# A two-layer gated MLP on one core: new order of first loads, filler transposes, a joint last block, and the last 96 features as one product

## The chip, the core and the metric

The kernel runs on one core of a Trainium2 chip. The core has five engines with instruction streams of their own: TensorE (PE, matrix products and transposes, with its weight loads shown apart as PEld), VectorE (DVE), ScalarE (ACT), GpSimd (POOL) and SyncE (SP). In this kernel SP issues every load and store, one after the other. Sums of products grow in PSUM banks, all other tiles lie in SBUF, and inputs, outputs and some intermediate arrays lie in DRAM.

The metric is the device time of one execution in microseconds (us), as a median over several runs. Besides these runs one execution is recorded by the profiler, and its rows are what "the profile" and "the trace" mean below.

## The reference, cut to what matters

The input x is 2048 tokens by 512 features (4 x 512 tokens). Two layers follow one another, and each adds to x the layer norm of what it computes from the layer norm of x.

```
def _L0_attn_ref(x, w_gate, w_up, w_down):
    s = silu(x @ w_gate.T)                       # 1376 features
    k = int(0.5 * I)
    _, idx = top_k(-abs(s), k)                   # the 688 smallest in magnitude of each row
    s[rows, idx] = 0
    s = s * (x @ w_up.T)
    return s @ w_down.T                          # back to 512

def _L0_ffn_ref(x, W_gate, W_up, W_down):
    return (silu(x @ W_gate.T) * (x @ W_up.T)) @ W_down.T

x = x + layernorm(_L0_attn_ref(layernorm(x), ...))
x = x + layernorm(_L0_ffn_ref(layernorm(x), ...))
```

All is in f32. The first layer thus needs, for each token, the median of 1376 magnitudes, and sets to zero what lies below it; the second layer has no such step.

## The kernel before, in words

Tokens are in 16 tiles of 128. The 1376 features are 10 groups of 128 and a last group of 96; the name `I` is 1376, `HF` is 640, so `2 * HF` is where the last 96 begin.

**Products with seven multiplications.** Most products are not made plainly. A product of matrices cut into 2 x 2 parts can be made with seven part products, where eight would be plain, if certain sums of parts are made first. `Seven` (L132) does that for products whose sums over the features are in PSUM: `first` makes products p1, p6, p5 in the banks pa, px, py; pa is copied out and px is added to the copy; `second` adds p7 to px and p2 to pa; `third` adds p4 to px and p3 to py. Because the banks go on being summed up, the copies and additions between these steps have to come in order. `stationary_sums` (L116) and `moving_sums` (L124) make the sums of parts for the side that TensorE holds and for the side that streams through it. `downs` (L233) does the same for the products with the down weights, with ten groups of 128 as two halves of five: its steps are p1, p5, p6 for each pair of tiles, then p7, p2, p4, p3, where each of the seven needs its own right side of 640 KB, loaded by `down_right` into a ring of three buffers. The last 96 features are added in `rest` (L263) by a plain matmul, for p7 in a bank of its own. Sums of weights that the second layer and the down products need are made once, early, by `presum` (L179), and lie in DRAM.

**Layer 1** (`Unit`, L348) goes by eight units of two tiles. For a unit, x is loaded and normalized, transposed on TensorE and copied out of PSUM by ScalarE (`normed_T`, L339); the gate product is made plainly in three column pieces of 464, 456 and 456 (L404), each followed on ScalarE by Silu (L408) and the magnitude (L409); the up product is a `Seven`. Then the threshold is searched: six passes of ScalarE over a tile with Sign and a sum (L456), each followed by small steps on VectorE, and an exact end (to L516). The masked product p is transposed on TensorE (`turns`, L578) and copied out by ScalarE (L582, L584), and then `downs` runs. These stages are offset: while unit j makes its gate and up products, unit j-1 is searched, unit j-2 is transposed and unit j-3 does its down products. `out_norm` (L321) takes statistics of the finished rows (`moments`, L98, ending with a power of -0.5 on POOL, L109), subtracts and scales on VectorE, adds x on POOL (L331) and stores.

**Layer 2** (`Block`, L624) goes by four blocks of four tiles. A block has five calls of `pair` (gate and up of 256 features, both as `Seven`), then `rest` (L674): gate and up of the last 96 features, 4 matmuls of 512 columns each into one bank for gate and one for up, Silu on ScalarE and a product on VectorE (L686). POOL makes the sums for the down products (`down_sums`). Then `finish` runs `downs` for the block's two pairs of tiles. In blocks 0 to 2 both pairs share a call, so that each right side is loaded once; in block 3 the first pair is finished, and then the second, each with its own seven loads. In the last call `final=True` lets `out_norm` take its statistics in two halves and do the last scaling and the addition of x in one instruction of VectorE (L328).

**The layer change** is where the two last units of layer 1 are searched, transposed and finished while the first block of layer 2 starts: the norms of block 0's first tiles and the loads of layer 2's weights are placed between the steps of unit 6 and unit 7. At its end a count of rows for which the search was not exact (`badi`) is made; after all work, every engine reads this count (L875) and jumps over a second, slower version of the whole computation (L876).

**What sets the order.** The code above is emitted in the order in which it is written, in `layers` (L721). Inside the block that L873 opens, a scheduler then orders each engine's instructions by its own estimate of times and dependences, so an edit at one place can reorder instructions at another. Buffers come from pools with a fixed number each: two PSUM banks for each of the tags pa, px, py and pt, three for the ring of down weights. At the start, 18 transposes of a constant (`warm`) run on TensorE before the first data is there.

## Time and profile before

| | us |
|---|---|
| three runs | 886.12, 888.31, 889.33 |
| median | 888.31 |
| the profiled execution | 887.46 |
| its span, first to last record | 885.5 |
| TensorE busy in it | 862.3 |
| VectorE, ScalarE, POOL busy | 511.8, 300.9, 180.3 |
| mean granted clock of TensorE | 0.993 |
| data moved | 117.54 MB |

The span is the time between the first and the last record of the profile; the device time of the same execution is 1.96 longer. An f32 matmul shows as two records, one after the other, because TensorE goes over f32 data in two passes; where a "pass" is spoken of, one record is meant. The granted clock is the share of full speed that TensorE was allowed in a stretch of time. "Waits" are idle times of an engine, put down to the instruction or transfer that released it. In a row such as `PE pg L404 <- ACT p L408: 2.5, 1, 2.5` TensorE waited at line 404 (output tile pg) for ScalarE's line 408 (output tile p), 2.5 us in sum, once, at most 2.5.

### The profile page before, as it was taken

To read this page: it belongs to the slowest core of one execution; us is meant where nothing else is said; L and a number is where in the kernel's file an instruction comes from. 1 tells how busy PE (TensorE), PEld (TensorE's weight loads), DVE (VectorE), ACT (ScalarE), POOL (GpSimd) and SP (SyncE) were. 2 spreads that over 40 slices of the span, in tenths; PEclk is the share of its full clock that TensorE was granted. 3 is DMA by queue.
4 is the path that set the end of the run, shared out by engine and by line. 5 is a ranking of instruction groups with operands and counts; after the bars stand their busy time and mean duration, and the time that the engine had idled before them with its cause. 6 is when DMAs were issued, how large, how long until landed. Compare 5 with 4: busy or idle time off the path is not lost. (4 is left out here: it accounts for less than half of the span.)

```text
span 885.5 us, 10211 instructions
## 1 busy us (share of the span) xinstructions
PE 862.3 (97%) x3588; PEld 652.4 (74%) x3588; DVE 511.8 (58%) x1328; ACT 300.9 (34%) x598; POOL 180.3 (20%) x249
## 2 busy tenths in 40 slices
PE   8999999999999899999999999999999999999995
PEld 5656566757667576677788888888788888888784
DVE  4887776775939578766955434554236443444322
ACT  2465575748463757466011111011101112011100
POOL 2120111212212112110433211321203221122221
PEclk9999999999999999999999999999999999999998
DMA  9999413334232343377374003610045002420064
GB/s 317 360 335 345 165 54 119 120 101 143 78 119 98 103 138 102 119 293 262 132 254 150 0 1 113 195 44 0 30 143 167 1 0 65 143 97 1 30 217 156
DMA packets 62924, 117.54 MB, mean 133 GB/s; under 512 B 4816, under 2 KB 36560, under 8 KB 62864
## 3 DMA queue, kind: packets, MB, share of 16 engines
q1 hardware_dynamic: 62864, 116.80, 39.4%
q8 instruction: 30, 0.49, 0.2%
q14 instruction: 30, 0.25, 0.1%
HBM read 97.91 MB, written 18.87 MB: 132 GB/s over the span
## 5 line engine op out<-in xcount | busy, mean ns | idle before, releaser
L456 ACT ACTIVATE ja<-v,cur 128x1376 bf16<-128x1376 f32 x96 | 138.3, 1441 | 76.9 <-DVE cur L481 54.4
L404 PE MATMUL pg<-wg,xT 128*128 128x456 f32 (+1 forms) x384 | 158.0, 559 | 3.4 <-ACT p L408 2.5
L404 PEld LDWEIGHTS pg<-wg,xT 128*128 128x128 f32 x384 | 73.2, 193 | 68.6 <-issue 59.9
L118 POOL TENSOR_TENSOR D<-hTb 128x256 f32<-128x256 f32 x20 | 14.6, 730 | 180.5 <-DVE hTb L672 180.5
L461 DVE TENSOR_SCALAR low<-cur 128x2 int32<-128x2 f32 x48 | 8.7, 181 | 72.0 <-ACT ja L456 72.0
L143 PE MATMUL pau<-wu,xT 128*128 128x344 f32 x128 | 43.6, 452 | 0.0
L143 PE MATMUL pagb<-xTb,wg 128*128 128x256 f32 x160 | 41.4, 379 | 0.0
L143 PE MATMUL paub<-xTb,wu 128*128 128x256 f32 x160 | 41.3, 380 | 0.0
L143 PE MATMUL pxub<-T,wu 128*128 128x256 f32 x160 | 41.2, 380 | 0.0
L143 PE MATMUL pxgb<-T,wg 128*128 128x256 f32 x160 | 41.1, 379 | 0.0
L258 PE MATMUL pad<-wd_p,hT 128*128 128x256 f32 x160 | 39.4, 380 | 1.3 <-DMA wd_p<-in_L_attn_w_down_dram 1.3
L408 ACT ACTIVATE p<-pg 128x456 f32<-128x456 f32 (+1 forms) x48 | 26.0, 544 | 43.1 <-PE pg L404 39.5
L258 PE MATMUL pxdb<-wdb_p,hTb 128*128 128x256 f32 x160 | 36.7, 379 | 2.1 <-DMA wdb_p<-sum_f 2.1
L258 PE MATMUL pxd<-wd_p,hT 128*128 128x256 f32 x160 | 37.2, 380 | 1.5 <-DVE y L293 1.5
L258 PE MATMUL padb<-wdb_p,hTb 128*128 128x256 f32 x160 | 37.1, 379 | 0.9 <-DMA wdb_p<-in_L_ffn_W_down_dram 0.9
L258 PE MATMUL pydb<-wdb_p,D 128*128 128x256 f32 x160 | 37.9, 379 | 0.1
L258 PEld LDWEIGHTS pxd<-wd_p,hT 128*128 128x128 f32 x160 | 30.3, 190 | 7.4 <-DVE y L293 1.7
L258 PEld LDWEIGHTS padb<-wdb_p,hTb 128*128 128x128 f32 x160 | 30.3, 190 | 7.2 <-issue 3.3
L258 PEld LDWEIGHTS pxdb<-wdb_p,hTb 128*128 128x128 f32 x160 | 30.3, 190 | 6.7 <-issue 2.5
L258 PEld LDWEIGHTS pad<-wd_p,hT 128*128 128x128 f32 x160 | 29.6, 190 | 7.4 <-DMA wd_p<-in_L_attn_w_down_dram 1.7
L258 PEld LDWEIGHTS pydb<-wdb_p,D 128*128 128x128 f32 x160 | 30.1, 190 | 6.2 <-issue 2.5
L670 ACT ACTIVATE sg<-sg 128x768 f32<-128x768 f32 x20 | 16.9, 843 | 50.9 <-DVE sg L167 50.9
(221 smaller groups left out, 1721.9 us busy)
## 6 DMA issues: line engine op xcount, KB each, us to landing
wd_p<-sum_a SPq DMA_DIRECT2D x28, 640.0 KB, 4.0
wd_p<-in_L_attn_w_down_dram SPq DMA_DIRECT2D x21, 640.0 KB, 4.2
wdb_p<-sum_f SPq DMA_DIRECT2D x20, 640.0 KB, 4.1
wdb_p<-in_L_ffn_W_down_dram SPq DMA_DIRECT2D x15, 640.0 KB, 4.2
xn<-in_x_dram SPq DMA_DIRECT2D x16, 256.0 KB, 3.1
xr<-in_x_dram SPq DMA_DIRECT2D x16, 256.0 KB, 2.8
x<-y SPq DMA_DIRECT2D x16, 256.0 KB, 2.0
xnb<-x SPq DMA_DIRECT2D x16, 256.0 KB, 3.1
```

The lines of the kernel that those rows point to most:

```text
L118: eng.tensor_add(s1, a21, a22)
L143: nc.tensor.matmul(ps, self.left[k][:, c, :], self.right[k][:, c, :], start=first and c == 0, stop=c == 1, skip_group_check=not first,)
L258: nc.tensor.matmul(p[which], p[1](k, c), ws[k][:, c, :], start=first and c == 0, stop=c == HC - 1, skip_group_check=not first,)
L404: nc.tensor.matmul(pg, self.xT[:, i, c, :], wg[:, c, c0:c1], start=(c == 0), stop=(c == NH - 1),)
L408: nc.scalar.activation(p[:, c0:c1], pg, AF.Silu)
L456: nc.scalar.activation(junk, v, AF.Sign, bias=cur[:, 0, i : i + 1], accum_out=cur[:, 1, i : i + 1],)
L461: nc.vector.tensor_scalar(low, cur[:, 1, :], 0.0, None, ALU.is_gt)
L670: nc.scalar.activation(sg[:, 1:, :], sg[:, 1:, :], AF.Silu)
```

## The change

There are six parts.

1. *First loads.* SP's order was x of tile 0, x of tile 1, and three column pieces of the gate weights. It becomes tile 0, the first piece, tile 1, and the two other pieces. Six filler transposes of tile 0's data, whose results nobody reads, are emitted after tile 0's norm.
2. *Order of sums in `downs`.* The addition of px (product p7) to yb's upper half is emitted right after p7, where it was emitted after p2; the rest of that sum becomes a step of its own, `c22`.
3. *Last block.* Its two pairs are made in one call of `downs`. The order of its end is p7, c22, p3, and then p4 and p2 of the first pair, p4 and p2 of the second. The last tile's `out_norm` takes its statistics for the first half straight from the PSUM bank of the p2 product and subtracts the mean by halves.
4. *The last 96 features.* Gate and up become one `Seven`: its 2 x 2 parts are gate and up on one side, two halves of the 512 input features, and two halves of the block's 512 tokens on the other. Its 14 matmuls have 256 columns. Three sums of the 96-column weights, made once on VectorE at the layer change (four instructions), go with it.
5. *Copies of transposed tiles.* For the unit before the last (`other`), the copies out of PSUM for its second tile go to VectorE in place of ScalarE.
6. *The count.* The read of `badi` and the jump are written inside the scheduled block. The read on SP thereby comes to stand in the layer change, after the load of x for tile 14's `out_norm` and before the load of tile 7 for layer 2; the other engines read it at their ends, as before.

With other edits the scheduler's estimate changes too, and the order in the middle of layer 1 is not the same as before, though none of its lines was edited.

```diff
-    def moments(src, nm, kind, n=1):
+    def moments(parts, nm, kind):
+        n = len(parts)
...
-        for i in range(n):
-            nc.vector.bn_stats(st[:, i, :], src[:, ts(i, H // n)])
+        for i in reversed(range(n)):
+            nc.vector.bn_stats(st[:, i, :], parts[i])
...
-        def product(k, which, i=None):
+        def product(k, which, i=None, part=slice(None)):
...
-            for p in [st[i]] if first else st:
+            for p in [st[i]] if first else st[part]:
...
         def p7():
             product("p7", PX)
             for p in st:
+                tiles, left, last, pa, px, py, ya, yb = p
+                nc.vector.tensor_add(yb[:, hi], yb[:, lo], px)
                 pz.append(bank("pt", f"pz{nm}_{p[0][0]}")[:, :H2])
                 rest(pz[-1], p, 1, hi, True)
 
-        def p2():
-            product("p2", PA)
+        def c22():
             for p, z in zip(st, pz):
                 tiles, left, last, pa, px, py, ya, yb = p
-                rest(pa, p, 0, lo)
-                nc.vector.tensor_add(yb[:, hi], yb[:, lo], px)
                 nc.vector.tensor_add(yb[:, hi], yb[:, hi], py)
                 nc.vector.tensor_add(yb[:, hi], yb[:, hi], z)
-                nc.scalar.copy(ya[:, lo], pa)
...
+        def p2(part=slice(None)):
+            product("p2", PA, None, part)
+            for p in st[part]:
+                tiles, left, last, pa, px, py, ya, yb = p
+                rest(pa, p, 0, lo)
+                if not final:
+                    nc.scalar.copy(ya[:, lo], pa)
+            if not final:
+                c22()
+            else:
+                for p in st[part]:
+                    tiles, left, last, pa, px, py, ya, yb = p
+                    if p is st[-1]:
+                        out_norm(work, tiles[0], ya, res, dst, nm, pa)
+                    else:
+                        nc.scalar.copy(ya[:, lo], pa)
+                        out_norm(work, tiles[0], ya, res, dst, nm)
...
-        return heads + [p7, p2, p4, p3]
+        if not final:
+            return heads + [p7, p2, p4, p3]
+        ends = [lambda f=f, i=i: f(slice(i, i + 1)) for i in range(len(pairs)) for f in (p4, p2)]
+        return heads + [p7, c22, p3] + ends
...
-        if final:
-            mv, rs = moments(y, f"o{nm}_{t}", "f", 2)
-            nc.vector.tensor_scalar(y, y, mv[:, 0:1], None, ALU.subtract)
+        if pa is not None:
+            parts = [pa, y[:, H2:]]
+            mv, rs = moments(parts, f"o{nm}_{t}", "f")
+            for i in range(2):
+                nc.vector.tensor_scalar(
+                    y[:, ts(i, H2)], parts[i], mv[:, 0:1], None, ALU.subtract
+                )
             nc.vector.scalar_tensor_tensor(y, y, rs, xr, ALU.mult, ALU.add)
...
-                nc.scalar.copy(hT[:, g0 : g0 + nf, :], pt[:, :nf, :])
+                copy = nc.vector.tensor_copy if other and k else nc.scalar.copy
+                copy(hT[:, g0 : g0 + nf, :], pt[:, :nf, :])
...
-            pg, pu = bank("pa", f"fg{nm}"), bank("px", f"fu{nm}")
-            for ps, w in ((pg, wg), (pu, wu)):
-                for c in range(NH):
-                    nc.tensor.matmul(
-                        ps[:n, :], w[:, c, 2 * HF :], self.xT[c // 2][:, c % 2, :],
-                        start=(c == 0), stop=(c == NH - 1),
-                    )
+            t = self.work.tile([P, 4, N2], F32, tag="w", name=f"sgr{nm}", bufs=1)[:n]
+            m = Seven(f"rb{nm}", left, self.right, t[:, 0, :], t[:, 1, :], t[:, 2, :])
+            m.first()
+            c11 = m.second()
             h = self.big.tile([P, N], F32, tag="b5", name=f"hTb{nm}_r")
-            nc.scalar.activation(h[:n, :], pg[:n, :], AF.Silu)
-            nc.vector.tensor_mul(h[:n, :], h[:n, :], pu[:n, :])
+            lo, hi = h[:n, :N2], h[:n, N2:]
+            nc.scalar.activation(lo, c11, AF.Silu)
+            m.third()
+            nc.scalar.activation(hi, m.c12, AF.Silu)
+            nc.vector.tensor_mul(lo, lo, m.c21)
+            nc.vector.tensor_mul(hi, hi, m.c22)
...
             units[0].norm(0)
+            if not general:
+                for i in range(6):
+                    nc.tensor.transpose(warm[:, i % 4, :], units[0].x[0][:, :P], ident)
+            wg = load_weight(wpool, a_wg, "wg", f"1{nm}", CH[:1])
             units[0].load(1)
-            wg = load_weight(wpool, a_wg, "wg", f"1{nm}", CH)
+            load_weight(wpool, a_wg, wg, f"1{nm}", CH[1:])
...
+            t = work.tile([P, 3, 2, I - 2 * HF], F32, tag="S", name=f"wrs{nm}", bufs=1)
+            rest = stationary_sums(
+                nc.vector,
+                *[w[:, 2 * c : 2 * c + 2, 2 * HF :] for w in ws for c in range(2)],
+                t[:, 0], t[:, 1], t[:, 2],
+            )
...
-                block.rest(*ws)
-                if last:
-                    block.finish([0], wr)
-                    block.finish([1], wr, True)
-                else:
+                block.rest(rest)
+                if not last:
                     for k in range(TB):
                         blocks[b + 1].norm(k)
                     blocks[b + 1].sums()
-                    block.finish([0, 1], wr)
+                block.finish([0, 1], wr, last)
...
-    nbad = nc.values_load(badi[0:1, 0:1], min_val=0, max_val=2 * P * NTT)
-    with tc.If(nbad > 0):
-        layers("g", True)
+        nbad = nc.values_load(badi[0:1, 0:1], min_val=0, max_val=2 * P * NTT)
+        with tc.If(nbad > 0, label="general"):
+            layers("g", True)
```

## The prediction

> **What bounds the kernel now.** I read the page's first part, then the busy time of each engine in six stretches chosen at the stage borders, then the waits of TensorE, then the timeline around each wait, and last the end of the span.
>
> ```profile
> PE 862.3 (97%) x3588; PEld 652.4 (74%) x3588; DVE 511.8 (58%) x1328; ACT 300.9 (34%) x598; POOL 180.3 (20%) x249
> ```
> TensorE is busy for 862.3 of 885.5 us. Only fewer matmul passes, fewer TensorE waits, a better clock, or a shorter head and tail can help.
>
> The stretches (start:end, length, then busy time per engine) are the start, layer 1, the layer change, layer 2, the last block's down products, and the tail:
>
> ```profile
> 0.00:22.00 22.00, 18.56 (x57) 11.04 (x58) 9.03 (x20) 6.48 (x15) 5.83 (x31) 0.92 0.93 318
> 22.00:410.00 388.00, 383.21 (x1431) 252.68 (x1430) 283.53 (x811) 230.41 (x434) 65.44 (x79) 1.00 0.49 166
> 410.00:470.00 60.00, 56.95 (x282) 49.00 (x281) 41.85 (x94) 10.44 (x30) 16.54 (x17) 1.00 0.65 216
> 470.00:841.20 371.20, 371.12 (x1677) 312.41 (x1677) 164.65 (x373) 52.40 (x118) 85.07 (x114) 1.00 0.21 67
> 841.20:876.90 35.70, 32.45 (x147) 27.27 (x145) 10.43 (x26) 1.12 (x3) 5.56 (x8) 1.00 0.64 214
> 876.90:885.50 8.60, 0.00 (x0) 0.00 (x0) 2.31 (x6) 0.00 (x0) 1.88 (x2) 0.63 0.20 70
> ```
> Layer 2 proper has no gap at all (371.12 of 371.20): there only the count of passes matters. The last block loses 35.70 - 32.45 = 3.25, the tail is 8.6 without a matmul.
>
> Who releases TensorE after its idle times (sum, times, longest):
>
> ```profile
> PE pg L404 <- ACT p L408: 2.5, 1, 2.5
> PE pxdb L258 <- DMA wdb_p<-sum_f: 2.1, 1, 2.1
> PE pxd L258 <- DVE y L293: 1.5, 1, 1.5
> PE ph L578 <- ACT hT L582: 1.4, 2, 1.1
> PE pad L258 <- DMA wd_p<-in_L_attn_w_down_dram: 1.3, 1, 1.3
> PE padb L258 <- DMA wdb_p<-in_L_ffn_W_down_dram: 0.9, 1, 0.9
> ```
> These few waits, 9.7 us together, are nearly all that is lost between start and tail. Two of them also cost clock. The granted clock in four stretches (last but two column):
>
> ```profile
> 5.31:8.72 3.41, 1.70 (x12) 1.04 (x11) 1.09 (x2) 1.29 (x4) 1.29 (x3) 1.00 1.03 388
> 8.72:12.14 3.42, 3.42 (x5) 1.64 (x6) 0.00 (x0) 0.00 (x0) 1.93 (x3) 0.50 1.04 398
> 295.44:298.86 3.42, 1.30 (x4) 0.70 (x5) 0.55 (x1) 3.33 (x6) 0.51 (x1) 1.00 0.00 0
> 298.86:302.27 3.41, 3.41 (x6) 1.62 (x5) 3.17 (x10) 2.18 (x8) 0.10 (x1) 0.50 0.00 0
> 862.06:865.47 3.41, 2.12 (x10) 1.52 (x8) 0.42 (x1) 0.00 (x0) 0.00 (x0) 1.00 0.92 271
> 865.47:868.88 3.41, 2.55 (x12) 2.30 (x13) 0.12 (x1) 0.00 (x0) 0.00 (x0) 1.00 1.06 404
> ```
> After a stretch of 3.41 us in which TensorE was busy for 1.70 or 1.30, the next stretch ran at clock 0.50; after 2.12 and 2.55 it did not. A half-clock stretch does half of its 3.41 us of work, so costs 1.7.
>
> **The change, part by part.** Everything is a difference to the profiled execution, 887.46 (span 885.5 and 1.96 around it).
>
> *First loads and fillers.* Tile 1's load moves behind the gate weights' first column piece, and the other two pieces behind tile 1. The queue's rows put half a microsecond on an issue, and the piece that the first gate product waits for (0.92 of wait at 8.63) comes one load of 256 KB earlier: estimate 0.5 to 0.7, so the product starts at about 8.0 and gains 0.6. Tile 0's statistics no longer run paired with tile 1's (two rows of 0.67), so its transposes start at about 5.7 instead of 6.38. Six filler transposes add 6 x 0.105 = 0.63 of work to a time in which TensorE waits anyway. In the stretch 5.31:8.72 TensorE is then busy for 0.32 (end of the warm-up) + 0.42 + 0.63 + 0.7 (the product) = 2.1, which stands beside the 2.12 that kept the clock. So 1.7 more, 2.3 in all; 0.6 if the clock falls anyway, -0.6 if the fillers delay the product. The later pieces land at about 11.0 and 13.3 and are needed at 11.6 and 14.7; tile 1's transposes come behind the first product at about 11.
>
> The Trainium skill, "TensorE: Matmul & The Clock Gate", section "What's actually happening", has the clock halve after at least one idle window of about 3.4 us, and its section "HAM oscillation" asks for no gaps over that. By that wording gaps of 0.74 and 0.92 couldn't have halved the clock and fillers would be worth nothing: the sum would be 1.7 smaller. The rows above disagree with the wording, since stretches half full halved it, so I go by the rows.
>
> *Rest as one product.* In layer 2 the last 96 gate and up features of a block were 8 matmuls of 512 columns in 2 passes each, 0.43 apart in the timeline: 16 x 0.43 = 6.88. They become 14 matmuls of 256 columns, 28 x 0.2147 = 6.01 (spacing of the 256-column passes of the down products). Saving 0.87, four times: 3.5. The new chain inside it (product, copy on ScalarE, add, product) is covered: down products of the same block stand between, 5.2 us of them before the second product that needs the chain, which is ready after about 2.2. Without that cover about 0.25 a block returns: 2.5. Some seven small VectorE and ScalarE instructions come in per block, where VectorE is busy for 44% of the stretch. The four sums of 96 columns at the layer change go to VectorE once, some 0.3 each.
>
> *Last block jointly.* Its two pairs of tiles share each weight load, so 7 loads of 640 KB replace 14; matmul count is unchanged. Both DMA waits there (0.94 and 2.15) came from a ring of three buffers fed by a queue that was moving 271 to 404 GB/s. With half the bytes for the same products the loads land 0.8 (p4), 1.5 (p7) and 3.7 (p2) us before they are needed: 3.1 gained, 2.5 if p4 is late by half a microsecond. Nothing is late next: 35.70 would become its busy 32.45.
>
> *Tail.* The 0.42 add that followed the last matmul goes, since the statistics read the last product where it lies. But the power on POOL follows POOL's own 1.26 add for the tile before, which ends at 878.05, so the chain behind it starts only 0.15 to 0.45 earlier. The read of the flag moves from the end of SP's queue into the layer change; at the end it stood alone:
>
> ```profile
> L875 SPq TENSOR_LOAD <-badi x1: 520/520/520, 880.2 to 880.2; - x1
> L875 SPq FUSED_REGOPS  x1: 186/186/186, 880.8 to 880.8; - x1
> SPq L876 <- SPq L876: 2.5, 1, 2.5
> ```
> 0.9 from 880.2 to the branch at 881.1, then 2.5 of waiting behind the branch (the first two rows from the flag read's instructions, the third from SP's waits). VectorE reads the flag too, and is through at 882.8, so of 0.9 + 0.3 about 1.1 shows; 0.2 if the 2.5 ends with the last store's landing (882.7) and not with the branch.
>
> *Layer 1.* Nothing is edited, but the order that the scheduler writes is another. The 2.48 wait at 297.56 was a gate product behind a Silu that stood behind two Sign passes of 1.44. In the changed order eight passes, about 2.8 us, stand between that product and its predecessor, so wait and half clock, 4.2, should go; elsewhere the neighbours of gate products change too. I take 2.5, the wait alone; from 5.2 (with the small ones of 0.2 to 0.5) to -4.2 (two new ones for the one).
>
> *Layer change.* Copies of transposed tiles move from ScalarE to VectorE (waits 1.12 and 0.24 there, 1.4 together); the add behind the 1.47 wait is issued one product earlier; but the norms of three tiles of layer 2 now stand on VectorE ahead of the last search steps, and one of those loads took 6.7 us to land. SP's flag read (0.9) queues ahead of the load for tile 7 and of the last unit's p2 weights; the flag is ready at 448.6, SP comes to it at 450.2, and the p2 load was issued only at 452.65, so it costs nothing there. The 1.31 wait on that load stays. I take 0.8, from 2.8 (1.4 + 1.4 of the 1.47) to -1.5 (one more wait like the 1.47).
>
> Sum: 2.3 + 3.5 + 3.1 + 1.1 + 2.5 + 0.8 = 13.3. 887.46 - 13.3 = 874.2. The median of the three runs is 888.31, 0.85 above the profiled execution, so the forecast is 875.0.
>
> **The rivals.**
> - *Clock halves at the start anyway.* The stretches' phase may differ, and 2.1 against 1.70 is a narrow bracket. Then 875.0 + 1.7 = 876.7.
> - *Layer 1 keeps its losses.* New gate waits replace the old: 875.0 + 2.5 = 877.5, with one more than before and its clock 881.7. For it: in the stretch 22:410 TensorE is busy for 99% with ScalarE at 59%, so a different order finds other tight places.
> - *VectorE is late at the layer change.* Three norms ahead of the search put it back by the 1.5 to 2.4 of one load: 877 to 878.
> - *The joint block or the rest doesn't give what it says.* If p4 and p7 are still late by 2 us together and the rest's chain shows in full (1.0): 878.
> - *Slower than before.* A gate product of layer 1 held by a Silu behind two Sign passes costs 2.5 + 1.7 = 4.2. Six units have this pattern, the old order was hit once. Layer 1 without its gain gives 877.5; three new waits beyond the old one bring 877.5 + 12.6 = 890.1, and from the fourth (894.3) the kernel is slower by more than 0.5%. Against it: in the changed order I find passes of other products between all but a few of them.
>
> **How the numbers follow.** Likeliest 875.0 with chance 0.42 (own range 872.5 to 877); start clock 0.12; layer 1 keeping its losses 0.18; layer change 0.10; block or rest 0.06; three or four more Silu waits 0.06; better than 872.5 by the upper ends (layer 1 at 5.2, layer change at 2.8) 0.06. Each gain by edited code (3.5 + 3.1 + 1.1 + 0.6 = 8.3) alone would give 880. The lower end 869.5 has the upper ends of layer 1 and the layer change (2.7 + 2.0) and of the run's spread; the upper end 882.5 has layer 1 with one new wait. What a measurement of this kernel can tell from no change is about 0.5%, 4.4 us: faster means below 883.9, chance 0.86; slower, above 892.8, 0.05, nearly all of the last rival; within, 0.09: what is left of it, and those parts of the cases of layer 1, the layer change and the block that fall together.
>
> **What would show it.** Right: passes of 256 columns in place of the 512-column ones, layer 2 without gaps and 3.5 shorter; seven down loads in the last block and no DMA wait over 0.5 there; clock 1.00 near 9 to 12 us; branch on SP right after the last store. Wrong: a gate wait over 2 us with a 0.50 stretch behind it; a wait on the search or on a tile's norm between 405 and 470 of more than 2; last products waiting for p4 or p2. The forecast falls if layer 1 has two or more such waits.

## The result, and the profile after

The changed kernel takes 886.69 us (median of 14 runs, 883.62 to 889.74), the kernel before 886.90 in its 14 (883.57 to 889.33): ratio 0.9996, 95% interval 0.998 to 1.0012. That is no change, where 875.0 was forecast and the range ended at 882.5. The profiled execution of the changed kernel took 885.25 (span 883.3), that of the kernel before 887.46 (885.5).

Five of the same six stretches in the changed kernel (start:end, length, busy time per engine, granted clock in the last but two column; the sixth, the tail, reaches beyond this span):

```profile
0.00:22.00 22.00, 20.05 (x76) 12.78 (x77) 10.30 (x21) 7.32 (x19) 5.68 (x31) 1.00 0.95 332
22.00:410.00 388.00, 378.51 (x1411) 248.55 (x1410) 284.86 (x803) 226.10 (x428) 65.13 (x79) 1.00 0.48 164
410.00:470.00 60.00, 57.42 (x279) 49.46 (x278) 43.41 (x107) 11.57 (x28) 15.39 (x16) 0.97 0.65 212
470.00:841.20 371.20, 371.10 (x1740) 323.89 (x1739) 171.69 (x396) 54.07 (x124) 86.66 (x116) 1.00 0.21 67
841.20:876.90 35.70, 30.93 (x144) 26.49 (x142) 14.37 (x37) 1.54 (x4) 5.99 (x7) 0.99 0.35 113
```

The first line improved (20.05 busy of 22.00, clock 1.00). The second got worse: TensorE now idles for 9.5 us in layer 1, where it idled for 4.8. Layer 2 is as full as it was, with fewer passes in it.

TensorE's waits in the changed kernel (sum, times, longest):

```profile
PE pg L432 <- ACT p L436: 2.9, 2, 1.5
PE pad L260 <- DMA wd_p<-in_L_attn_w_down_dram: 2.2, 1, 2.2
PE pxu L144 <- DVE c L154: 1.8, 1, 1.8
PE pau L144 <- ACT c L153: 1.0, 1, 1.0
PE ph L606 <- ACT he L613: 0.8, 1, 0.8
PE pyd L260 <- DVE D L630: 0.8, 1, 0.8
PE pxu L144 <- DVE c L160: 0.7, 1, 0.7
PE pad L260 <- DVE p L454: 0.5, 1, 0.5
```

The two transfer waits of the last block are gone, and so is the one of 2.5 in layer 1. But instead of that one there are now eight smaller ones, on ScalarE and VectorE (`ph` and `pyd` had counterparts before, of 1.1 and 0.8; the other six are new), and the wait on the p2 weights at the layer change (L260, `pad`, released by a DMA) grew from 1.3 to 2.2.

Matching places in the two profiled executions give a ladder:

| place in TensorE's order | before | after | difference | its change |
|---|---|---|---|---|
| first up product | 29.74 | 26.96 | -2.78 | -2.78 |
| first transpose of layer 2 | 410.54 | 411.75 | +1.21 | +3.99 |
| product ahead of the p2 wait | 455.48 | 455.16 | -0.32 | -1.53 |
| last 96-feature product of layer 1 | 469.16 | 471.39 | +2.23 | +2.55 |
| end of the last matmul | 876.82 | 872.13 | -4.69 | -6.92 |
| end of the span | 885.5 | 883.3 | -2.2 | +2.49 |

The start gave 2.8 and layer 2 gave 6.9, and all of it was lost again at three places: layer 1 (4.0), the p2 wait (2.55), the tail (2.5). What remains, 2.2, is one execution's; the medians differ by 0.2.

The p2 wait in two stretches of 3.41 us, of which the second follows the first:

```profile
456.05:459.46 3.41, 1.22 (x6) 0.98 (x6) 2.09 (x6) 0.00 (x0) 0.55 (x1) 1.00 0.79 284
459.46:462.87 3.41, 3.41 (x10) 2.71 (x9) 0.14 (x1) 0.00 (x0) 0.73 (x1) 0.50 0.01 6
```

TensorE was busy for only 1.22 of the first, and the second ran at clock 0.50, the same pattern as twice in the kernel before. So in this execution a wait that grew by 0.9 cost 0.9 + 1.7.

The tail in the changed kernel, in order of time (start, length, instruction; in brackets the idle time ahead of it and what ended it):

```profile
868.73 0.34 SPq L360 DMA_DIRECT2D out_dram<-yb  x1
869.12 0.42 SPq L348 DMA_DIRECT2D xrb<-x  x1
...
871.75 0.38 PE L266 MATMUL padb<-wr,hTb_r 96*128 96x256 f32 x1
...
873.07 0.15 DVE L108 TENSOR_SCALAR ve_ob<-mv_ob 128x1 f32<-128x1 f32 x1
...
873.65 1.35 POOL L359 TENSOR_TENSOR yb<-yb,xrb 128x512 f32<-128x512 f32 x1 [1.77 <-DVE ve_ob L108]
874.96 0.54 POOL L110 TENSOR_TENSOR rs_ob<-ve_ob,nhalf 128x1 f32<-128x1 f32 x1
875.02 1.63 SPq L360 DMA_DIRECT2D out_dram<-yb  x2
875.54 0.75 DVE L356 SCALAR_TENSOR_TENSOR yb<-yb,rs_ob,xrb 128x512 f32<-128x512 f32 x1 [1.66 <-POOL rs_ob L110]
```

The last tile's variance is ready at 873.22, but its power on POOL begins at 874.96: it stands behind POOL's addition for the tile before, and that addition began only at 873.65. The residual that it adds (`xrb`) was loaded at 869.12, behind the store at 868.73, and landed 4.1 later, at 873.2. VectorE then idles 1.66. In the kernel before, the addition for the tile before the last followed VectorE by 0.66:

```profile
876.79 1.26 POOL L331 TENSOR_TENSOR yb<-yb,xrb 128x512 f32<-128x512 f32 x1 [0.66 <-DVE yb L114]
```

### The profile page after: what moved, and what is told of

It reads as the page before. It is cut to its first block, busy times and chain, and to the rows that moved or that the text cites. A ratio compares the mean times of both kernels' runs of the same rounds, so it can differ in the third digit from the quotient of the medians.

```text
span 883.3 us, 10345 instructions
## 1 busy us (share of the span) xinstructions
PE 858.0 (97%) x3642; PEld 661.2 (75%) x3642; DVE 524.6 (59%) x1361; ACT 300.6 (34%) x601; POOL 178.8 (20%) x249
## 4 chain that ended last, share of the span: by engine, by line
PE 50%; DVE 16%; issue 6%; ACT 5%; DMA 2%; POOL 1%; SPq 0%; POOLq 0%; ACTq 0%; DVEq 0%
PE pxgb L144 6%; PE pxub L144 6%; ACT ja L484 5%; PE pxdb L260 4%; PE pyub L144 4%; PE pagb L144 4%; PE paub L144 4%; PE pygb L144 4%; PE padb L260 3%; PE pydb L260 3%; PE pg L432 2%; DVE p L538 2%; DVE ext L522 2%; PE pxd L260 2%; PE pyd L260 1%
## 5 line engine op out<-in xcount | busy, mean ns | idle before, releaser
L432 PE MATMUL pg<-wg,xT 128*128 128x456 f32 (+1 forms) x384 | 154.8, 549 | 2.9 <-ACT p L436 2.9
L260 PE MATMUL pad<-wd_p,hT 128*128 128x256 f32 x160 | 40.7, 390 | 2.7 <-DMA wd_p<-in_L_attn_w_down_dram 2.2
L260 PE MATMUL pydb<-wdb_p,D 128*128 128x256 f32 x160 | 37.8, 380 | 0.0
L260 PE MATMUL pxd<-wd_p,hT 128*128 128x256 f32 x160 | 37.3, 380 | 0.0
L260 PE MATMUL padb<-wdb_p,hTb 128*128 128x256 f32 x160 | 36.7, 379 | 0.0
L260 PE MATMUL pxdb<-wdb_p,hTb 128*128 128x256 f32 x160 | 36.2, 379 | 0.0
L260 PEld LDWEIGHTS pad<-wd_p,hT 128*128 128x128 f32 x160 | 30.0, 194 | 8.3 <-DMA wd_p<-in_L_attn_w_down_dram 2.6
L260 PEld LDWEIGHTS pxd<-wd_p,hT 128*128 128x128 f32 x160 | 30.7, 192 | 4.9
L144 PEld LDWEIGHTS pau<-wu,xT 128*128 128x128 f32 x128 | 23.7, 191 | 13.9 <-issue 2.8
L260 PEld LDWEIGHTS padb<-wdb_p,hTb 128*128 128x128 f32 x160 | 30.5, 190 | 4.2
L260 PEld LDWEIGHTS pxdb<-wdb_p,hTb 128*128 128x128 f32 x160 | 30.4, 190 | 4.2
```

What stands on the lines that cost most here:

```text
L144: nc.tensor.matmul(ps, self.left[k][:, c, :], self.right[k][:, c, :], start=first and c == 0, stop=c == 1, skip_group_check=not first,)
L260: nc.tensor.matmul(p[which], p[1](k, c), ws[k][:, c, :], start=first and c == 0, stop=c == HC - 1, skip_group_check=not first,)
L432: nc.tensor.matmul(pg, self.xT[:, i, c, :], wg[:, c, c0:c1], start=(c == 0), stop=(c == NH - 1),)
```

## The experiments

Each diff is against the changed kernel, unless it says otherwise. All ratios are to the kernel before, measured beside it on the same chip.

### What the new start costs layer 1

`old_start`: the first loads in the old order, no fillers.

```diff
-            if not general:
-                for i in range(6):
-                    nc.tensor.transpose(warm[:, i % 4, :], units[0].x[0][:, :P], ident)
-            wg = load_weight(wpool, a_wg, "wg", f"1{nm}", CH[:1])
             units[0].load(1)
-            load_weight(wpool, a_wg, wg, f"1{nm}", CH[1:])
+            wg = load_weight(wpool, a_wg, "wg", f"1{nm}", CH)
```

> The changed kernel, only with the first loads in the old order and without the filler transposes. TensorE's order in layer 1 is then nearly that of the kernel before. Theory A (the new start itself gains 2.8 us, and the other order of layer 1 that comes with it loses 4.0): TensorE reaches the first up product at about 29.7 instead of 26.96, idle time of TensorE between 22 and 410 us falls from 9.5 to about 4.8; median 1 below the changed kernel's, 885.5. Rival B (layer 1 loses time for a reason that is not its order, say the other copies or the sums): idle time there stays at 9 or more and the start's 2.8 are lost on top; 889.5.

Measured: 882.54, ratio 0.9966 (0.9944 to 0.9988). Layer 1's waits of this kernel between 22 and 410 us are the old list:

```profile
PE pg L432 <- ACT p L436: 2.5, 1, 2.5
PE ph L606 <- ACT hT L611: 1.1, 1, 1.1
PE pyd L260 <- DVE D L630: 0.8, 2, 0.4
PE pxu L144 <- DVE c L160: 0.2, 1, 0.2
```

TensorE is busy for 371.43 of the 375 us from 30 to 405 (before: 371.42, changed kernel: 366.32), and that although one half-clock stretch was there again, as in the kernel before. The first up product comes at 29.45. So theory A holds for the mechanism: layer 1 lost its time through the order that the scheduler wrote, which changed because the start changed. Its size was more than expected: taking the new start out gained 0.3% (about 2.7 us), not 1, though with seven runs its interval still touches that of the changed kernel (0.998 to 1.0012).

`before_start`: the reverse, the kernel before with the new loads and the fillers alone (the lines with a minus above, put into the kernel before).

> The kernel before with the new order of first loads and the fillers alone. Theory A (gain of 2.8 at the start, loss of 4.0 in layer 1 through the other order that the scheduler writes there): the first up product starts at about 27, TensorE's idle time between 22 and 410 us is about 9.5, median 886.9 + 1.2 = 888.1. Rival B (layer 1 loses nothing by it): 884.1.

Measured: 892.91, ratio 1.0076 (1.0049 to 1.0104), worse than either theory. The first up product comes at 26.86 and layer 1 has the changed kernel's order, with 366.72 busy of 375, as theory A said. But in addition the layer change got worse, in its waits from 405 to 470 us:

```profile
PE pxd L258 <- DMA wd_p<-sum_a: 2.9, 1, 2.9
PE pad L258 <- DMA wd_p<-in_L_attn_w_down_dram: 2.8, 2, 1.9
```

with half-clock stretches behind two of them (417 and 465 us), and a third in layer 1, behind a wait of 2.2 on the search (73 us). The p7 product comes earlier in this order than its weights land.

`no_fill`: the changed kernel without the six fillers, with the new order of loads.

```diff
-            if not general:
-                for i in range(6):
-                    nc.tensor.transpose(warm[:, i % 4, :], units[0].x[0][:, :P], ident)
```

> The changed kernel without the six filler transposes. Theory A (the fillers keep the clock in the first stretches; each other emission gives another order in layer 1 with other waits): the clock halves once near 8 to 12 us, first up product at about 28.7 in place of 26.96, and TensorE's idle time between 22 and 410 us is another one than 9.5 or 4.8; median 886 to 890. Rival B (the fillers are worth nothing for the clock): first up product at about 27, no half-clock stretch before 20 us.

Measured: 888.16, ratio 1.0009 (0.9994 to 1.0025). The time is in theory A's range, but the part on the fillers is rival B's: no half clock before 20 us, first up product at 26.93 as with the fillers. In the stretch 5.31:8.72 TensorE is busy for 2.92 without fillers (3.18 with them), since the first product begins at 7.04 already. What made the start faster is the order of the loads. The third order of layer 1 has its own waits (1.75, 1.92 with a half-clock stretch, 1.51, 1.03).

### The read of the count

`load_end`: the read and the jump behind all work again.

```diff
-        nbad = nc.values_load(badi[0:1, 0:1], min_val=0, max_val=2 * P * NTT)
-        with tc.If(nbad > 0, label="general"):
-            layers("g", True)
+    nbad = nc.values_load(badi[0:1, 0:1], min_val=0, max_val=2 * P * NTT)
+    with tc.If(nbad > 0, label="general"):
+        layers("g", True)
```

> The changed kernel, only with the read of the count put back behind all work, as before the change. Theory A (the read stands on SP ahead of the load of the p2 weights at the layer change and makes that load late): the wait of TensorE at that product falls from 2.19 us to about 1.3, the half-clock stretch behind it (1.7) goes, SP's read costs 0.9 at the end again; median 1.7 to 2.6 below the changed kernel's 886.7, so 884 to 885. Rival B (the load is late for another reason, its 5.16 us in flight): the wait stays at about 2.2 and the half clock too, the end is 0.9 longer; 887.6.

Measured: 885.55, ratio 0.9991 (0.9974 to 1.0009). SP's issues show the mechanism of theory A. In the changed kernel the count is read at 451.6 and SP goes on at 452.75:

```profile
451.19 0.39 SPq L348 DMA_DIRECT2D xr<-in_x_dram  x1
452.75 0.33 SPq L364 DMA_DIRECT2D xnb<-x  x1
453.18 0.38 SPq L231 DMA_DIRECT2D wd_p<-in_L_attn_w_down_dram  x1
```

and without the read there:

```profile
450.77 0.39 SPq L348 DMA_DIRECT2D xr<-in_x_dram  x1
451.22 0.44 SPq L364 DMA_DIRECT2D xnb<-x  x1
451.91 0.38 SPq L231 DMA_DIRECT2D wd_p<-in_L_attn_w_down_dram  x1
```

The load of the p2 weights (`wd_p`) is issued 1.14 us after the load of `xr`, two places ahead of it, instead of 1.99. The wait fell to 1.74 (1.3 was expected), no half-clock stretch came, and TensorE ended layer 1 2.55 us earlier (468.84 against 471.39). 1.7 of that is the clock. In the times little shows (0.05% between the two ratios): the half-clock stretch is not there in every execution.

Nor does layer 1 end early whenever it is missing. In three other runs with the read at the same place (`pad30`, `old_sum`, `res_pad`) there is no half-clock stretch, but TensorE waits 1.7 at 451 us for a bank that the count occupies, and layer 1's last product comes at 471.55 to 471.83, as late as in the changed kernel (471.39). In `pad30`:

```profile
PE pz L266 <- DVE badi L887: 1.7, 1, 1.7
```

Kernels that read the count behind all work have this wait too (`best2` 1.31, `best3` 1.58), so it does not come from the read; what sets it stays open.

### Layer 2 alone, and the tail

`layer2_only`: the kernel before, with the product of the last 96 features and the joint last block, and nothing else of the change (diff against the kernel before, its core).

```diff
-                block.rest(*ws)
-                if last:
-                    block.finish([0], wr)
-                    block.finish([1], wr, True)
-                else:
+                block.rest(rest)
+                if not last:
...
-                    block.finish([0, 1], wr)
+                block.finish([0, 1], wr, last)
```

> The kernel before with two parts of the change alone: the last 96 features as one product and the last block made jointly with its new end. First loads, copies, order of sums at the layer change and place of the read are the old ones. Theory A (these two parts are worth what the passes and the two transfer waits come to, 6.9 us, and the tail behind the last matmul grows by 1.7 to 2.5 because the residuals' loads come late): 886.9 - 6.9 + 2.1 = 882.1, the last matmul 6.9 earlier than in the kernel before. Rival B (the parts are worth little and what the last matmul gains in the changed kernel comes from elsewhere): 885 to 887.

Measured: 884.30, ratio 0.9978 (0.9965 to 0.9991). From the last product of layer 1 to the last matmul it needs 401.27 (before 407.66, changed kernel 400.74), and no transfer wait is left in layer 2; so the 6.4 to 6.9 are real. The tail takes 11.7 where it took 8.68, and eats 3.0. In this execution the clock was halved for three stretches of 3.41 us as well. The expected 882.1 was 2 too low, the direction and place are those of theory A.

`res_early`: the last block's four residuals are loaded ahead of its down products, in buffers that are free by then.

```diff
+        if final:
+            for n, t in enumerate(t for p in pairs for t in p[0]):
+                kw = dict(tag="xn", bufs=3) if n < 2 else dict(tag="xr")
+                early[t] = work.tile([P, H], F32, name=f"xr{nm}_{t}", **kw)
+                nc.sync.dma_start(early[t], res[ts(t, P), :])
...
-        xr = work.tile([P, H], F32, tag="xr", name=f"xr{nm}_{t}")
-        nc.sync.dma_start(xr, res[ts(t, P), :])
+        xr = early.pop(t, None)
+        if xr is None:
+            xr = work.tile([P, H], F32, tag="xr", name=f"xr{nm}_{t}")
+            nc.sync.dma_start(xr, res[ts(t, P), :])
```

> The changed kernel, only with the four residuals of the last block loaded at the start of its down products, into buffers of their own. Theory A (in the tail, POOL's addition for the tile before the last waits for a residual whose load stood on SP behind a store, and POOL's power for the last tile waits behind that addition): the addition starts about 1.1 us earlier against the last matmul, the gap of 1.66 in front of the last VectorE instruction shrinks to about 0.5, the tail goes from 11.2 to about 10; median 885.5. Rival B (POOL is late for another reason, or the end is set by something that does not wait for the last store): tail stays at 11.2.

Measured: 884.93, ratio 0.9982 (0.9966 to 0.9998). The timeline of its tail:

```profile
871.89 1.26 POOL L368 TENSOR_TENSOR yb<-yb,xrb 128x512 f32<-128x512 f32 x1 [0.66 <-DVE yb L115]
873.11 0.60 POOL L110 TENSOR_TENSOR rs_ob<-ve_ob,nhalf 128x1 f32<-128x1 f32 x1
873.74 0.75 DVE L365 SCALAR_TENSOR_TENSOR yb<-yb,rs_ob,xrb 128x512 f32<-128x512 f32 x1 [0.44 <-POOL rs_ob L110]
```

With the last matmul ending at 871.48, the addition begins 0.4 after it (1.5 in the changed kernel) and VectorE's gap is 0.44 in place of 1.66. The tail is 10.02 in place of 11.17: theory A, and its size. The times alone would not show it, since the intervals of this run and of the changed kernel overlap.

A second loss remained behind it, between SP's last instructions. In `res_early` SP's eight event instructions behind the branch stretch over 2.2 us, where they take 0.5 in the kernel before:

```profile
L922 SPq EVENT_SEMAPHORE  x8: 17/17/17, 877.9 to 880.1; - x8
```

In the changed kernel these eight take 0.5 (879.9 to 880.4), and the hole lies among the next eight: four are done at 880.7, the other four come from 882.1 on.

```profile
L947 SPq EVENT_SEMAPHORE  x4: 28/28/28, 880.5 to 880.7; - x4
L947 SPq EVENT_SEMAPHORE  x4: 28/28/28, 882.1 to 882.3; - x4
```

So it is 1.4 long. The 2.0 of the two expectations that follow is the way from 880.4 to the first drain instruction at 882.4, with these eight counted in. `pad30` moved the code behind the branch without touching what is executed:

```diff
             if general:
+                for i in range(30):
+                    nc.sync.dma_start(flags[:, 0, :1], x[:P, :1])
                 wr = last_rows(a_wd, 1)
```

> The changed kernel, only with 30 small loads added on SP in the second version that is never executed. What runs is the same; the instructions behind it move by some 34 places in SP's program, about to where they lay in the kernel before. Theory A (the 2.0 us between SP's event instructions behind the branch, at 880.5, and its next instruction, at 882.4, are the fetch of instructions that lie across a border, because the joint block took loads out of SP's program): the gap falls to 0.5 as before, the tail from 11.2 to about 9.7. Rival B (the gap waits for something that is really done then, a landing or another engine): it stays at 1.9 to 2.1.

Measured: 886.16, ratio 0.999 (0.9978 to 1.0002), tail 11.23. On SP the hole is gone: its sixteen events run from 880.6 to 881.6, and two drains are done at 881.7. Then SP waits 1.9 for other engines, which all meet at the end of the kernel (drains and waits, from the rows of L949):

```profile
L949 SPq DRAIN  x3: 7/7/13, 881.7 to 883.7; - x3
SPq L949 <- PEq L949: 2.4, 2, 1.9
L949 DVEq DRAIN  x2: 10/72/135, 883.3 to 883.8; - x2
```

The last to come is VectorE: its event behind the branch is at 880.9, its first drain only at 883.3 (TensorE's first is at 873.6, POOL's at 877.7). The changed kernel has this second stall too, at the same time as SP's:

```profile
L913 DVEq EVENT_SEMAPHORE  x1: 21/21/21, 880.1 to 880.1; - x1
L947 DVEq DRAIN  x2: 10/72/134, 882.5 to 882.9; - x2
```

So theory A held for SP's hole, and the tail stayed at 11.2 for a reason that neither theory had: two engines stall side by side until 882.1 and 882.5, and padding SP's program takes away one of the two stalls. `res_pad` is `res_early` with 20 such loads (`range(20)`), which puts the instructions as far up as in the kernel before.

> The changed kernel with the residuals of the last block loaded early, as in the run of that alone, and 20 small loads in the version that is never executed, which put the instructions behind the branch at the place in SP's program where the kernel before had them. Theory A (the 2.0 us between SP's last instructions are a fetch across a border of its program): no gap over 0.6 us between SP's events at the end, tail from 10.0 to about 8.0. Rival B (it waits for something that happens at the end): the gap of 2.0 stays somewhere, tail 10.

Measured: 882.96, ratio 0.9961 (0.9945 to 0.9977). The first row is of the branch's line, the second of the end of the kernel:

```profile
L924 SPq EVENT_SEMAPHORE  x8: 17/17/17, 879.0 to 879.5; - x8
L958 SPq DRAIN  x3: 7/7/13, 880.1 to 880.4; - x3
```

No hole; the tail is 8.34, 1.7 less than in `res_early` and 2.8 less than in the changed kernel. VectorE does not stall in these two runs (event and drain at 878.2 and 878.3 in `res_early`, 879.4 and 879.5 here; why, no run isolates), so SP's hole alone decides between them, and code that never runs takes it away. What theory A forecast came. The other runs agree: a second hole of 1.3 to 1.6 on SP is there in all eight kernels with the joint block and without such loads, in neither of the two with the old block, and in none of the four with such loads. It is no wait for a landing: in `res_early` the last store lands 2.5 after its issue at 874.5, about 877.0, and the hole begins at 878.4. That it is the fetch of instructions is the reading that is left; no record names it. With the tail mended alone, the whole change measures 0.4% faster than the kernel before (against `res_early` the intervals overlap).

### The two small edits of the layer change

`act_copies`: all copies of transposed tiles on ScalarE.

```diff
-                copy = nc.vector.tensor_copy if other and k else nc.scalar.copy
+                copy = nc.scalar.copy
```

> The changed kernel, only with all copies of transposed tiles on ScalarE, as before the change. Theory A (the copies on VectorE are worth the part of the 1.12 wait at 406 us that went, and little more): the wait there goes from 0.77 back to about 1.1, the time stays within 1 us of the changed kernel's 886.7. Rival B (the copies load VectorE at a place where the search needs it and are themselves a loss): 1.5 to 3 us faster, 884.

Measured: 888.33, ratio 1.0023 (1.0011 to 1.0036), so the copies on VectorE are worth about 0.27%, 2.4 us against the changed kernel's ratio. Neither theory had this. The wait at 407 us stays 0.78; what comes in is the wait of 2.69 for p7's weights at 416 us that `before_start` had, with a half-clock stretch. The scheduler gave the layer change another order, in which p7 comes ahead of its weights.

`old_sum`: the addition of px behind p2 again.

```diff
         def p7():
             product("p7", PX)
             for p in st:
-                tiles, left, last, pa, px, py, ya, yb = p
-                nc.vector.tensor_add(yb[:, hi], yb[:, lo], px)
...
         def c22():
             for p, z in zip(st, pz):
                 tiles, left, last, pa, px, py, ya, yb = p
+                nc.vector.tensor_add(yb[:, hi], yb[:, lo], px)
                 nc.vector.tensor_add(yb[:, hi], yb[:, hi], py)
```

> The changed kernel, only with the addition of px issued behind the p2 product again, as before the change. Theory A (the earlier addition is what took the 1.47 wait at 433 us away): a wait of about 1.5 on that addition comes back at 430 to 436 us, 888. Rival B (it went with the other order of the layer change): no such wait, 886.7.

Measured: 886.56, ratio 1.0006 (0.9994 to 1.0017), no wait on that addition anywhere from 405 to 470. Rival B: the 1.47 wait went with the other order of the layer change, and the edit itself is worth nothing here.

### Put together

`best2`: the edits of `old_start`, `load_end` and `res_early`, 19 small loads in the version that never runs, and a longer warm-up.

```diff
-    for i in range(18):
+    for i in range(24):
         nc.tensor.transpose(warm[:, i % 4, :], ident, ident)
```

> Meant to beat both: the changed kernel with the first loads in the old order, six more transposes of the constant in the warm-up in place of the fillers (emitted ahead of the scheduled block, so that layer 1 stays close to its old order), the read of the count behind all work, residuals of the last block loaded early, and 19 small loads in the version that is never executed. Theory A (the losses that the runs showed are separate and each goes with its cause): no half clock at the start (-1.7 to -3.4), p2 wait at the layer change 1.3 to 1.7 without half clock, tail about 9: 886.9 - 6.9 (layer 2) - 1.7 (start) - 1.0 (layer change) + 0.5 (tail) = 877.8. Rival B (other orders bring other waits): 881 to 883.

Measured: 881.26, ratio 0.9937 (0.9916 to 0.9959). No half clock in this execution, tail 8.97, p2 wait 1.40. Still there are the 2.48 wait of the old layer 1, a wait of 1.31 for the gate weights at the start, and one of 1.31 at 449 us for a bank that the count occupies, as in `old_start` (1.32).

`best3`: the same, with the new order of loads, 30 transposes in the warm-up and 15 small loads.

```diff
-    for i in range(24):
+    for i in range(30):
...
-            units[0].load(1)
-            wg = load_weight(wpool, a_wg, "wg", f"1{nm}", CH)
+            wg = load_weight(wpool, a_wg, "wg", f"1{nm}", CH[:1])
+            units[0].load(1)
+            load_weight(wpool, a_wg, wg, f"1{nm}", CH[1:])
```

> Meant to beat the combination that was the fastest so far: the same, with the changed kernel's order of first loads, without fillers, and with 30 transposes of the constant in the warm-up, a number for which the scheduler writes layer 1 almost in its old order. Theory A (the new order of loads gains at the start, and what it lost came from the order of layer 1 alone): first product at about 7.9 in place of 9.28, first up product at about 27.5, idle time between 22 and 410 us about 5 to 6; 880. Rival B (the loads' order itself disturbs what follows): 883 to 886.

Measured: 881.24, ratio 0.9931 (0.991 to 0.9953). The start gives what theory A said (first product at 7.56, first up product at 27.45, 1.2 earlier than in `best2`), and TensorE is busy for 369.60 of 375 in layer 1. It comes back at the layer change (waits of 1.58 and 1.79) and in one half-clock stretch at 298 us. `best2` stayed 3.5 above its 877.8 and `best3` 1.2 above its 880; both beat both kernels by about 0.6%.

## Why the prediction was wrong

**Right.** *Rest as one product* and *last block jointly*: 3.5 + 3.1 = 6.6 was the sum, 6.92 came in the profile, and `layer2_only` has 6.4. *First loads*: 2.3 was the sum, 2.78 came, though not as I had it: my 2.3 gave 1.7 to the fillers keeping the clock and 0.6 to the loads, while `no_fill` shows that the new loads alone bring the first product to 7.04 and keep the clock.

**Layer 1: the term +2.5 was -4.0.** This is the step that failed most: 6.5 of the 11.1 by which the profiled sum falls short. I priced the one large wait that would go and took for new waits only the same kind, a gate product behind two Sign passes with its half clock, in counts of 4.2. Of this kind two came, smaller and without half clock: gate products at 129 and 356 us wait 1.42 and 1.52 for a Silu that stands behind Sign passes of 1.44. Four more of 0.5 to 1.8, 4.0 together, are of kinds I had no term for: on additions and copies of the up product (`c`) and on its multiplication into `p`. The largest, 1.8 at 226 us, is an addition that comes on VectorE after an instruction of the search of 1.64 (L519). Idle time rose by 4.7 and the half-clock stretch, 1.7, went; the remaining 1.0 of the 4.0 is longer busy time, which no run explains. The lower bound of -4.2 was nearly reached. The order before was better than a fresh one: the one other fresh order (`no_fill`) idles as much, and from 30 to 405 us the kernels with the old order or one close to it idle for 3.0 to 5.4 us, all others for 7.3 to 9.3. I had treated the scheduler's new order as neutral with a gain on top. The rival "layer 1 keeps its losses" was the nearest, with 877.5 to 881.7.

**The half clock.** I took 1.7 each at two places from one execution. That execution had a mean clock of 0.993. Among 82 further executions of the kernel before, 20 had 0.993 or less (median 887.4) and 22 had 0.997 or more (885.0); the median one is between. So the kernel as usually measured had only part of the 3.4 to give. The forecast also added 0.85 for a median of three runs, 888.31; fourteen have 886.90.

The rows of the prediction, with the clock lost after 1.70 and 1.30 busy of 3.41 us and kept after 2.12 and 2.55, are right, but the busy time of a stretch does not decide alone. In the changed kernel this stretch, in step with the two above (it lies 69 stretches ahead of 459.46), was busy for 1.59 and kept the clock:

```profile
223.94:227.35 3.41, 1.59 (x7) 1.07 (x7) 3.41 (x10) 0.65 (x2) 0.00 (x0) 1.00 0.27 77
227.35:230.77 3.42, 2.90 (x17) 2.21 (x16) 3.42 (x12) 1.07 (x2) 0.55 (x1) 1.00 0.00 0
```

**Layer change: +0.8 was -1.0.** The first part, copies and order, gave 1.53. "It costs nothing there" is the wrong sentence. I compared SP's arrival at the read (450.2) with the issue of the p2 load in the profile before (452.65) and took the 2.4 between as room. SP came to the read at 451.6 only, was through 1.15 later, and the load went out 0.85 later after the load of `xr` than in `load_end`. Against the kernel before it went out 0.53 later (453.18 and 452.65), and TensorE came to its product 0.32 earlier: these two make the 0.9. In the profiled execution the clock then halved; in `res_early`, with the read at the same place, it did not after a wait of 2.21. The read's worth over many executions is therefore not settled: `load_end` differs from the changed kernel by 0.05%, inside both intervals.

**Tail: +1.1 was -2.5.** I looked for what the edit shortens and saw POOL's addition as the cover, without asking what that addition waits for. In the old end POOL's addition followed VectorE by 0.66 us, its residual was there; in the joint end four tiles finish within about 10 us and share two residual buffers and one queue, so a residual's load stands behind a store that stands behind POOL. `res_early` prices that at 1.15. The read did leave SP's end, 0.9, but I took the 2.5 behind the branch as given and had no term for a stall after it. Against the last matmul, the last store is issued 1.2 later than before, the branch follows it 0.9 sooner, SP's first event behind the branch comes after 3.1 in place of 2.5, and from there to the end it takes 3.5 in place of 1.9: 1.2 - 0.9 + 0.6 + 1.6 = 2.5. Of the last part 1.4 is SP's hole, with a stall on VectorE beside it. The joint block took loads out of SP's program, and as the padded runs show, where its end then lies decides about the hole; `res_pad` prices it at 1.7.

The sum of the profiled ladder is then 2.78 - 3.99 + 1.53 - 2.55 + 6.92 - 2.49 = 2.2 (13.3 expected). The medians show 0.2: the profiled execution of the changed kernel lies 1.4 below its median, that of the kernel before 0.6 above.

The Trainium skill, "TensorE: Matmul & The Clock Gate", section "What's actually happening", has the clock halve after an idle window of about 3.4 us. This doesn't fit the changed kernel either: a stretch busy for 1.22 of 3.41 us, with a longest gap of 2.19, was followed by 0.50. That the fillers were worth nothing, as one reads from it, came out all the same, for another reason: without them the stretch was busy for 2.92.

## What to carry to other kernels

In a kernel whose instructions a scheduler orders, an edit at the start is an edit everywhere: compare the orders first, and price a new order of a nearly full stage as a loss to be bounded by the idle time that other orders show, not as a free draw. Look at the end of a program as a chain of its own, with its loads, its queue and its code on every engine, before crediting what the last matmul gains. And price a clock loss by how often it occurs over executions, not by the one that was profiled.

## What was not expected of the hardware

The time of SP behind a taken branch depends on where the code lies: some 2.5 to 3.1 us pass in every run before its first instruction there, and after that the same instructions ran through or stood still at one of them, for 1.4 in the changed kernel and 1.6 in `res_early`; 20 or 30 instructions that never run decided which. VectorE has such a stall of its own, 2.3 us in the changed kernel, and one can hide the other. A wait for a transfer of 2.2 was followed by a half-clock stretch, worth 1.7, in one execution and by none in another (`res_early`). And the read of a value by SP held its queue for about 1.1 us at the layer change, 734 ns of it in the read itself, which had taken 520 at the end of the kernel before.
